# Gate products on 32 columns of the array, the latent by halves of the tokens on 64 columns, and an order of the work drawn per stretch of steps

## The chip, the cores and the metric

The kernel runs on one core of a Trainium2 chip. It uses five engines: TensorE (PE in the profile; its weight loads are listed apart as PEld), VectorE (DVE), ScalarE (ACT), GpSimd (POOL), and SyncE (SP), which only issues transfers here. The metric is the device time in microseconds of one execution; lower is better. A time is the median of several executions, and one more execution is recorded by the hardware profiler.

## The reference

Eight sequences of 512 tokens with 256 features go through four residual layers, all in float32:

```
x = x + attention_a(layernorm(x));  x = x + ffn(layernorm(x))
x = x + retention_b(layernorm(x));  x = x + ffn(layernorm(x))

attention_a:  q = x Wq + bq;  latent = x Wd + bd  (64 wide);  k, v = latent Wup + bup;  16 heads of 16, rope on q and k
   out = softmax(q k' / 4 + distance terms) v
   out = out + 0.2 * sigmoid(q . mean_k) * mean_v        # mean over the 512 tokens
   return out Wo + bo
retention_b:  q, k, v = projections;  return ((q k') * decay) v        # no softmax
ffn:          relu(x W1 + b1) W2 + b2                                   # 1024 wide
```

## The kernel before, in words

**Layout.** The tokens of a sequence are 4 tiles of 128 (`NT`), the features 2 chunks of 128 (`NC`). The heads are handled in 4 groups of 4 (`NG`); a head takes 32 partitions, 16 for its dimensions and the rest for helper rows, so that four heads fill the array's rows.

**Front of a sequence.** `front1` and `front2` normalise x, turn it (`xT`), and make the `lat` tile, keys, queries and values from it. In the kernel before, `latent` multiplies with the weights `wd_sb` laid out twice side by side, so that the 64 latent features stand on partitions 0 to 63 and once more on 64 to 127, both for all 512 tokens. The keys (`k`) read one copy per half of the head dimension (`e`), the values (`v`) one copy per odd and even token tile; so two matmuls of 64 rows can stand side by side on the array's rows. `half_unit` adds bias and rope on VectorE, `rotate` combines the halves on GpSimd, `stripes` copies them by transfers of SP into `qT` and `kT`. `mean_k` writes `kmean`, `gate` multiplies `kmean` (16 useful columns of 128) with the rotated queries and writes tanh of it into 16 rows of `gates`. `mean_v` and `through_wo` make `mem`, 17 rows: what each head's mean value gives behind Wo, and a row of constants. `wo_unit` adds `gates` times `mem` to the output projection. (sigmoid is written with tanh, so a constant row of ones in `gates` carries the rest.)

**Attention steps.** There are 256 steps, 32 per sequence, and 6 more that close the pipeline. One step multiplies scores of two heads twice: `s` (queries on partitions, for the row maxima, read by VectorE into `mr`) and, 12 steps behind (`LAG`), `t` (keys on partitions, read by ScalarE's exp into `p`). The decay factors `dec_a` are multiplied on GpSimd, or VectorE where the planner says so. `pv` multiplies `p` with the values, on 32 columns per head. The tiles `s` and `t` share two PSUM buffers.

**The rest of a sequence** (`rest`, `rest_last`): output projection (`wo`), the feed-forward layers (`hx` up, `x` down), retention (`b`, `bv`, `bs`, `bo`), with three layer norms (f, r, g).

**What sets the order.** Every engine runs its instructions in program order. `plan` (a function at build time) writes that order: it keeps a clock for each engine, takes the costs from the `Unit` objects (`Unit(latent, 1720, ...)`: 1720 ns of TensorE, then 700 ns of ScalarE, and so on), and puts units of work between the steps. It is run for 144 rules (reserve, lateness and so on); the rule with the smallest cost is emitted. It adds 1700 ns to a plan's cost for each wait of TensorE over 1200 ns, and during the first two sequences fills waits over 700 ns with matmuls that nothing uses (`warm`).

Lines L69 and L203 in the profile are the helpers that record instructions (`traced` and `mm`), L206 is `flip` (turns on TensorE), L93 is `move` (transfers of SP).

Of the kernel before, what the change touches and what calls it, by code (L numbers as in the profile page):

```python
# [35 lines left out]
def tile_kernel(  # L36
# [80 lines left out]
    wd_sb = keep([P, NC, 2, LAT], "wd_sb")  # L117
    for j in range(2):
        move(wd_sb[:, :, j, :], wdown)
# [30 lines left out]

    gates = [keep([P, T], f"ga{i}") for i in range(2)]
    mem = [keep([P, D], f"me{i}") for i in range(2)]
    bo_row = keep([32, D], "bo_row")
    kmean = keep([P, 2, P], "kmean")
    vmean = keep([P, NC, P], "vmean")
    hmask = keep([P, NH], "hmask")
    vmask = keep([P, NC, NH + 1], "vmask")
# [3 lines left out]
    def memory_buffers():  # L161
        for i in range(2):
            gps.memset(gates[i], 0.0)
            gps.memset(mem[i], 0.0)
        gps.memset(bo_row, 0.0)
        gps.memset(vmean, 0.0)
        gps.memset(vmask, 0.0)
        gps.memset(vmask[:, :, NH : NH + 1], 1.0)
        gps.memset(kmean, 0.0)

    def masks():
        dve.reduce_sum(hmask, ident.rearrange("p (h d) -> p h d", d=HH), axis=AX.X)
        for c in range(NC):
            dve.reduce_sum(
                vmask[:, c, c * HH : (c + 1) * HH], ident.rearrange("p (h d) -> p h d", d=HD), axis=AX.X
            )
        gps.tensor_scalar(hmask, hmask, 0.5 / T, None, ALU.mult)

    late = {}

    def loads_before_scores():
        xs[1] = load_x(1)
        late["dec_a"] = resident(decay_a, "dec_a")
        for i in range(2):
            move(gates[i][NH : NH + 1, :], rope[HD : HD + 1, 0, :])
        move(bvc, rows[0:D].rearrange("(c p) -> p c", p=P))

    def late_loads():
        move(bo_row[NH : NH + 1, :], rows[D : 2 * D].unsqueeze(0))

        for g in range(NG):
            at_row = (g % 2) * 4 * HD
            move(wo_sb[at_row : at_row + 4 * HD, g // 2, :], wo.rearrange("(h d) g n -> h d g n", d=32)[:, :HD, g, :])

        move(wvu[:, :, :D], wb[:, :, 2, :])
        late["w1"] = resident(w1, "w1_sb")
        late["w2"] = resident(w2, "w2_sb")
        late["dec_b"] = resident(decay_b, "dec_b")
# [21 lines left out]
    wk_sb = keep([P, P], "wk_sb")  # L220

    def regroup_k():
        for e in range(2):
            act.copy(
                wk_sb[e * LAT : (e + 1) * LAT, :].rearrange("p (h d) -> p h d", d=HH),
                wk_in[e * LAT : (e + 1) * LAT, :, e * HH : (e + 1) * HH],
            )
# [8 lines left out]
    pick = keep([P, 2, 32], "pick")  # L236
# [20 lines left out]
    AHEAD = 6  # L257
# [152 lines left out]
    def front1(b):  # L410
        def latent(part=0, parts=1):
            if part == 0:
                lat_a[b] = fr.tile([P, T], F32, tag="lat", name=f"lat_{b}")
                lsum[b] = fr.tile([P, 2], F32, tag="lsum", bufs=1, name=f"lsum_{b}")
            ps = misc(f"lat_{b}_{part}")
            n = T // parts
            cols = slice(part * n, (part + 1) * n)
            for c in range(NC):
                mm(ps[:, :n], wd_sb[:, c].rearrange("p j n -> p (j n)"), xT_a[b]["xT"][:, c, cols], c == 0, c == NC - 1)
            act.activation(  # L420
                lat_a[b][:, cols], ps[:, :n], AF.Identity,
                bias=bd, accum_out=lsum[b][:, part : part + 1],
            )
            if part == 1:
                gps.tensor_add(lsum[b][:, 0:1], lsum[b][:, 0:1], lsum[b][:, 1:2])
# [3 lines left out]
        def values():  # L429
            ps = [misc(f"v_{b}_{j}") for j in range(2)]  # L430
            for i in range(2):
                for j in range(2):
                    rows_of = slice(j * LAT, (j + 1) * LAT)
                    t = 2 * i + j
                    mm(ps[j][:, i * D : (i + 1) * D], lat_a[b][rows_of, t * P : (t + 1) * P], wv_sb[rows_of])
            for j in range(2):
                act.copy(
                    vaug[b % 2][:, j::2, : NH * 17].rearrange("p i (h d) -> p i h d", d=17)[:, :, :, :HD],
                    ps[j].rearrange("p (i h d) -> p i h d", i=2, d=HD),
                )  # L440


        def mean_v():
            ps = misc(f"mv_{b}")
            for c in range(NC):
                mm(ps[:, c : c + 1], wv_sb[:LAT, c * P : (c + 1) * P], lsum[b][:LAT, 0:1])
            m = fr.tile([P, NC], F32, tag="mv_a", name=f"mv_a_{b}")
            dve.scalar_tensor_tensor(m, ps[:, :NC], 0.1 / T, bvc, ALU.mult, ALU.add)
            for c in range(NC):
                gps.tensor_scalar(vmean[:, c, : NH + 1], vmask[:, c, :], m[:, c : c + 1], None, ALU.mult)  # L450

        def bias_through_wo():
            ps = misc("bo")
            for c in range(NC):
                mm(ps[:, :D], vmean[:, c, :], wo_sb[:, c, :], c == 0, c == NC - 1)
            dve.tensor_add(bo_row[: NH + 1, :], ps[: NH + 1, :D], bo_row[: NH + 1, :])

        def through_wo():
            ps = misc(f"me_{b}")
            for c in range(NC):  # L460
                mm(ps[:, :D], vmean[:, c, :], wo_sb[:, c, :], c == 0, c == NC - 1)
            dve.tensor_add(mem[b % 2][: NH + 1, :], ps[: NH + 1, :D], bo_row[: NH + 1, :])

        s, (h0, h1) = ln_units(lambda: xs[b], f"a{b}", fr)
        u = {"lat": Unit(latent, 1720, (("ACT", 700),), after=[h0[2], h1[2]]), "latent": latent}
# [16 lines left out]
    def front2(b, u1):  # L482
# [3 lines left out]
        def projected(j, e):  # L486
            ps = misc(f"{'qk'[j]}{e}_{b}")
            if j == 0:
                for c in range(NC):
                    mm(ps, wq_sb[:, c, e, :], xT_a[b]["xT"][:, c, :], c == 0, c == NC - 1)  # L490
            else:
                rows_of = slice(e * LAT, (e + 1) * LAT)
                mm(ps, wk_sb[rows_of], lat_a[b][rows_of])
            return ps

        def keys():
            ps = [projected(1, e) for e in range(2)]
            for e in range(2):
                half_unit(1, e, ps[e])

        def half_unit(j, e, ps, order="cs"):
            for n in order:
                table = cos if n == "c" else nsin
                if b == 0 and (j, e) == (0, 1):
                    if not spare:
                        spare["t"] = at.tile([P, 2, T], F32, tag="p", bufs=PB, name="rq1_0")
                    t = spare["t"][:, "cs".index(n), :]
                else:
                    t = fr.tile([P, T], F32, tag="rot", bufs=6, name=f"r{n}{j}{e}_{b}")
                dve.scalar_tensor_tensor(t, ps, qk_bias[:, j, e : e + 1], table, ALU.add, ALU.mult)  # L510
                rot[n, j, e] = t
# [28 lines left out]
        def gate():  # L540
            ps = misc(f"ga_{b}")
            for e in range(2):
                mm(ps, kmean[:, e, :], rot[0, e], e == 0, e == 1)
            act.activation(gates[b % 2][:NH, :], ps[:NH, :], AF.Tanh)
# [4 lines left out]
        k = [Unit(keys, 950, rope + rope, after=[lat], bank=2)]  # L549
        kt = Unit(lambda: turn(1), then=(("POOL", 2800),), after=k, step=free)  # L550
        km = Unit(mean_k, then=(("ACT", 1300), ("POOL", 1400)), after=[kt])
        q = [Unit(lambda e=e: half_unit(0, e, projected(0, e)), 1720, rope, after=[lat]) for e in range(2)]
        qt = Unit(lambda: turn(0), then=(("POOL", 2800),), after=q, gives=("qk", b))
        ga = Unit(gate, 1720, (("ACT", 600),), after=[km, qt], needs=(("wo", b - 2),))
# [5 lines left out]
        if b == 0:  # L560
            return projected, half_unit, rotate, stripes, [km, u1["v"], ga, u1["mv"], u1["me"]]
# [465 lines left out]
    projected, half_unit, rotate, stripes, order0 = front2(0, front[0][1])  # L1027
# [20 lines left out]
    latent(0, 2), latent(1, 2)  # L1048
    regroup_k()
    regroup_q(1)  # L1050
    half_unit(0, 0, projected(0, 0))
    k_ps = [projected(1, e) for e in range(2)]
    half_unit(1, 0, k_ps[0]), half_unit(1, 1, k_ps[1], "sc")
    rotate(1, 0, gps), rotate(1, 1, gps)
    half_unit(0, 1, projected(0, 1), "sc")
# [8 lines left out]
    gps.tensor_copy(vmean[:, :, NH], bvc)  # L1064
# [7 lines left out]
    def plan(reserve, later, early, fast, lead, bias, emit=False):  # L1072
# [196 lines left out]
        valued, drawn = [0], [0]  # L1269
        shifts, posts = [], []  # L1270
# [36 lines left out]
        while t < LAST or any(chains) or posts or shifts or valued[0] < NS:  # L1307
            while True:
# [7 lines left out]
                for c, u in ready:  # L1316
                    if (u is c[0] or u.norm) and start_of(u) is not None:
                        c.remove(u)
                        issue(u)
            s_step = step_start(t) if t < LAST else None  # L1320
# [4 lines left out]
            for rank, c in enumerate([shifts, posts] + chains):  # L1325
# [11 lines left out]
                if t >= LAST:  # L1337
                    key = (max(s - (BONUS if c is last_two[0] or c is last_two[1] else 0), clock["PE"] + 50), -rank)
                if best is None or key < best[0]:
# [24 lines left out]
            if best is not None and not take:  # L1364
                soon = clock["PE"] + 50
                take = (best[1] is posts or best[1] is shifts or credit > 0) and best[2] <= max(soon, s_step)
# [28 lines left out]
    plan(*min(rules, key=cost.get), emit=True)  # L1395
# [109 lines left out]
```

## Time and profile before

| what | value |
|---|---|
| median of 3 runs (lowest, highest) | 1268.3 us (1267.91, 1269.02) |
| the profiled execution's own time | 1267.68 us |
| its span, first to last instruction | 1265.9 us |
| its mean granted TensorE clock | 0.995 |
| HBM read, written | 13.92 MB, 4.43 MB |

The profile's first part gives busy time per engine, its second cuts the span into 40 slices with the busy share in tenths, its fourth follows the chain of work that ended last, its fifth groups instructions by tile. In the trace a float32 matmul stands as two passes (records), so a group's count is twice the number of matmuls; a matmul that turns a tile (L206) is one pass. The timeline view gives start, length, engine, operation and count, with the wait ahead of it in brackets.

### The profile page before, as it was taken

To read this page: it belongs to the slowest core of one execution; us is meant where nothing else is said; L and a number is where in the kernel's file an instruction comes from. 1 tells how busy PE (TensorE), PEld (TensorE's weight loads), DVE (VectorE), ACT (ScalarE), POOL (GpSimd) and SP (SyncE) were. 2 spreads that over 40 slices of the span, in tenths; PEclk is the share of its full clock that TensorE was granted. 3 is DMA by queue.
4 is the path that set the end of the run, shared out by engine and by line. 5 is a ranking of instruction groups with operands and counts; after the bars stand their busy time and mean duration, and the time that the engine had idled before them with its cause. 6 is when DMAs were issued, how large, how long until landed. Compare 5 with 4: busy or idle time off the path is not lost.

```text
span 1265.9 us, 15939 instructions
## 1 busy us (share of the span) xinstructions
PE 1225.4 (97%) x6168; PEld 628.8 (50%) x6168; DVE 615.4 (49%) x995; ACT 499.4 (39%) x746; POOL 763.6 (60%) x699
## 2 busy tenths in 40 slices
PE   7989999999998999999999999999999999999999
PEld 5423445344534344455443644535543554467777
DVE  4777854573544663345734365433634372232410
ACT  2245444444453434334335245343434334523131
POOL 4379965795766876676657576675656564731210
PEclk9999999999999999999999999999999999999999
DMA  5310010002100100010000200011000100000000
GB/s 136 117 39 23 23 38 6 14 7 56 29 14 5 49 23 18 18 48 23 1 14 5 66 22 14 1 31 41 4 5 14 31 5 5 26 1 1 1 5 30
DMA packets 32728, 31.94 MB, mean 25 GB/s; under 512 B 14065, under 2 KB 23538, under 8 KB 32372
## 3 DMA queue, kind: packets, MB, share of 16 engines
q1 hardware_dynamic: 31740, 30.13, 8.7%
q8 instruction: 49, 0.80, 0.3%
q10 hardware_dynamic: 912, 0.79, 0.2%
q14 instruction: 27, 0.22, 0.1%
HBM read 13.92 MB, written 4.43 MB: 14 GB/s over the span
## 4 chain that ended last, share of the span: by engine, by line
PE 88%; DVE 6%; POOL 2%; DMA 2%; ACT 1%; issue 1%; SPq 0%; ACTq 0%; DVEq 0%
PE hx L203 19%; PE s L203 18%; PE x L203 18%; PE pv L203 8%; PE wo L203 3%; PE bs L203 3%; PE bo L203 3%; DVE mr L69 3%; PE b L203 2%; PE bv L203 2%; PE q L203 2%; POOL p L69 2%; PE t L203 2%; PE warm L203 1%; PE lat L203 1%; PE ga L203 1%
## 5 line engine op out<-in xcount | busy, mean ns | idle before, releaser
L69 POOL TENSOR_TENSOR p<-p,dec_a 128x512 f32<-128x512 f32 x482 | 610.0, 1290 | 296.5 <-ACT p L69 290.1
L69 DVE TENSOR_REDUCE mr<-s 128x2 f32<-128x1024 f32 x256 | 312.7, 1223 | 314.0 <-PE t L203 291.6
L69 ACT ACTIVATE p<-t 128x1024 f32<-128x1024 f32 (+1 forms) x282 | 263.0, 944 | 366.0 <-PE t L203 356.3
L203 PE MATMUL s<-kT,qT 32*128 32x512 f32 x1024 | 289.3, 640 | 19.5 <-DVE mr L69 17.0
L203 PE MATMUL t<-qT,kT 32*128 32x512 f32 x1024 | 287.2, 641 | 0.5 <-ACT p L69 0.3
L203 PE MATMUL x<-w_sb,h_x 128*128 128x256 f32 x960 | 221.0, 384 | 0.0
L203 PEld LDWEIGHTS x<-w_sb,h_x 128*128 128x128 f32 x960 | 178.3, 190 | 59.4 <-issue 36.4
L203 PEld LDWEIGHTS s<-kT,qT 32*128 32x128 f32 x1024 | 78.0, 183 | 162.0 <-DVE mr L69 62.9
L203 PE MATMUL pv<-p,va 128*32 128x512 f32 x1024 | 132.8, 608 | 1.6 <-ACT num L69 0.7
L69 ACT ACTIVATE h_x<-hx,vec 128x512 f32<-128x512 f32 (+1 forms) x128 | 84.5, 660 | 109.2 <-PE hx L203 108.3
L203 PE MATMUL hx<-xT_f,w_sb 128*128 128x512 f32 (+1 forms) x288 | 122.1, 560 | 0.2 <-ACT xT_f L69 0.2
L203 PE MATMUL hx<-xT_g,w_sb 128*128 128x512 f32 (+1 forms) x288 | 122.0, 560 | 0.0
L69 DVE TENSOR_TENSOR x<-x,x 128x256 f32<-128x256 f32 x60 | 25.5, 425 | 153.2 <-PE x L203 145.7
L203 PEld LDWEIGHTS t<-qT,kT 32*128 32x128 f32 x1024 | 78.6, 183 | 14.2 <-ACT p L69 5.4
L203 PEld LDWEIGHTS hx<-xT_g,w_sb 128*128 128x128 f32 x288 | 51.2, 189 | 64.0 <-issue 60.1
L203 PEld LDWEIGHTS hx<-xT_f,w_sb 128*128 128x128 f32 x288 | 50.8, 189 | 64.3 <-issue 55.3
L203 PEld LDWEIGHTS pv<-p,va 128*32 128x32 f32 x1024 | 25.3, 109 | 77.1 <-issue 51.5
L69 POOL TENSOR_TENSOR x<-x,b 128x256 f32<-128x256 f32 x60 | 43.9, 754 | 14.7 <-DVE xn_g L69 11.6
L69 POOL TENSOR_TENSOR rc<-rc,rs 128x512 f32<-128x512 f32 x30 | 40.2, 1361 | 9.2 <-DVE rs L69 9.2
L69 DVE TENSOR_TENSOR p<-p,dec_a 128x512 f32<-128x512 f32 x30 | 35.7, 1227 | 18.1 <-ACT p L69 18.1
L69 POOL TENSOR_TENSOR rstd_g<-ve_g,half 128x2 f32<-128x2 f32 x16 | 11.3, 704 | 54.0 <-DVE ve_g L69 53.8
L69 ACT COPY num<-pv 128x512 f32<-128x512 f32 x32 | 18.7, 585 | 57.9 <-PE pv L203 53.4
(172 smaller groups left out, 1103.0 us busy)
## 6 DMA issues: line engine op xcount, KB each, us to landing
kT<-rc SPq DMA_DIRECT2D x64, 64.0 KB
qT<-rc SPq DMA_DIRECT2D x60, 64.0 KB
x<-in_x_dram SPq DMA_DIRECT2D x7, 512.0 KB
aT<-num SPq DMA_DIRECT2D x112, 32.0 KB
rec<-d_rec SPq DMA_DIRECT2D x14, 256.0 KB
out_dram<-x SPq DMA_DIRECT2D x28, 128.0 KB
w_sb<-in_w_dram SPq DMA_DIRECT2D x2, 1024.0 KB
x<-in_x_dram SPq DMA_DIRECT2D x2, 256.0 KB
```

Of the source, the lines that this page charges most:

```text
L69: ins = f(*a, **k)
L203: tc.keep_in_program_order(nc.tensor.matmul(o, lhsT=l, rhs=r, start=start, stop=stop))
```

## The change

It has four parts.

1. **Latent.** `wd_sb` is held once instead of twice. For each chunk, two matmuls of 256 tokens stand on 64 columns each: the first half of the tokens goes to partitions 0 to 63, the second half to 64 to 127. `lat` is 256 wide instead of 512. The keys are made by `projected_keys`: four matmuls of 256 columns (two `e` by two token halves) instead of two of 512, and each key tile is read from two PSUM tiles, so `half_unit` runs twice as many VectorE instructions of half the width for keys. Sums for mean v come from one accumulator column on 128 partitions, so an addition on GpSimd falls away. The first sequence keeps its two parts, one per half of the tokens.
2. **Gate.** `kmean` has 32 columns. `gate` issues eight matmuls of 128 tokens (two `e` by four token tiles), each token tile on its own 32 columns, instead of two of 512 tokens on 128 columns; then four tanh of 32 partitions by 128 columns instead of one of 16 by 512. `gates` becomes block-diagonal by token tile, and `mem`, `vmask`, `vmean`, `bo_row` hold their 17 rows four times. The constant ones come from the bias of tanh (`one_rows`: 40 in that row) instead of a transfer into each gate tile.
3. **Planner's costs.** Latent 1050 instead of 1720 ns, gate 620 instead of 1720, keys one entry of 3500 ns on VectorE instead of two of 1550, the ScalarE parts of latent and gate 480 and 900 instead of 700 and 600.
4. **Draws.** After the best rule is found, each stretch of 16 steps (`min(t, LAST) // 16`, 17 stretches) is given a number from 1 to 6 in turn, which seeds a random generator. Where a stretch has one, candidates' start times get 0, 400 or 1500 ns added by chance (0 three times in five), and the threshold of the credit that lets work in before a step gets 0, 1500 or -1500. A number is kept if the planner's cost of the whole plan falls. The emitted plan uses the kept numbers.

In the program as built, the number of matmuls per kind stays the same except for `lat` (18 to 32), `k` (16 to 32), `ga` (16 to 64) and `warm` (76 to 92). 482 decay products are on GpSimd and 30 on VectorE in both.

```
-    wd_sb = keep([P, NC, 2, LAT], "wd_sb")
-    for j in range(2):
-        move(wd_sb[:, :, j, :], wdown)
+    wd_sb = keep([P, NC, LAT], "wd_sb")
+    move(wd_sb, wdown)
...
+    one_rows = keep([P, 4], "one_rows")
-    kmean = keep([P, 2, P], "kmean")
+    kmean = keep([P, 2, 32], "kmean")
-    vmask = keep([P, NC, NH + 1], "vmask")
+    vmask = keep([P, NC, NT, 32], "vmask")
...
     def loads_before_scores():
         xs[1] = load_x(1)
         late["dec_a"] = resident(decay_a, "dec_a")
-        for i in range(2):
-            move(gates[i][NH : NH + 1, :], rope[HD : HD + 1, 0, :])
+        move(one_rows, blocks[:, P : P + 4])
...
-        def latent(part=0, parts=1):
-            if part == 0:
-                lat_a[b] = fr.tile([P, T], F32, tag="lat", name=f"lat_{b}")
-                lsum[b] = fr.tile([P, 2], F32, tag="lsum", bufs=1, name=f"lsum_{b}")
-            ps = misc(f"lat_{b}_{part}")
-            n = T // parts
-            cols = slice(part * n, (part + 1) * n)
+        def latent(parts=(0, 1)):
+            if parts[0] == 0:
+                lat_a[b] = fr.tile([P, T // 2], F32, tag="lat", name=f"lat_{b}")
+                lsum[b] = fr.tile([P, 1], F32, tag="lsum", bufs=1, name=f"lsum_{b}")
+            ps = misc(f"lat_{b}_{parts[0]}")
+            n = T // 2
             for c in range(NC):
-                mm(ps[:, :n], wd_sb[:, c].rearrange("p j n -> p (j n)"), xT_a[b]["xT"][:, c, cols], c == 0, c == NC - 1)
-            act.activation(
-                lat_a[b][:, cols], ps[:, :n], AF.Identity,
-                bias=bd, accum_out=lsum[b][:, part : part + 1],
-            )
-            if part == 1:
-                gps.tensor_add(lsum[b][:, 0:1], lsum[b][:, 0:1], lsum[b][:, 1:2])
+                for j in parts:
+                    mm(
+                        ps[j * LAT : (j + 1) * LAT, :n], wd_sb[:, c, :], xT_a[b]["xT"][:, c, j * n : (j + 1) * n],
+                        c == 0, c == NC - 1,
+                    )
+            at_ = slice(parts[0] * LAT, (parts[-1] + 1) * LAT)
+            act.activation(lat_a[b][at_], ps[at_, :n], AF.Identity, bias=bd[at_], accum_out=lsum[b][at_])
...
             for c in range(NC):
-                gps.tensor_scalar(vmean[:, c, : NH + 1], vmask[:, c, :], m[:, c : c + 1], None, ALU.mult)
+                gps.tensor_scalar(vmean[:, c, :], vmask[:, c].rearrange("p t h -> p (t h)"), m[:, c : c + 1], None, ALU.mult)
...
-        u = {"lat": Unit(latent, 1720, (("ACT", 700),), after=[h0[2], h1[2]]), "latent": latent}
+        u = {"lat": Unit(latent, 1050, (("ACT", 480),), after=[h0[2], h1[2]]), "latent": latent}
...
-            else:
-                rows_of = slice(e * LAT, (e + 1) * LAT)
-                mm(ps, wk_sb[rows_of], lat_a[b][rows_of])
...
+        def projected_keys():
+            ps = [misc(f"k{j}_{b}") for j in range(2)]
+            n = T // 2
+            for e in range(2):
+                for j in range(2):
+                    rows_of = slice(j * LAT, (j + 1) * LAT)
+                    mm(ps[j][:, e * n : (e + 1) * n], wk_sb[rows_of, e, :], lat_a[b][rows_of])
+            return [[p[:, e * n : (e + 1) * n] for p in ps] for e in range(2)]
...
-                dve.scalar_tensor_tensor(t, ps, qk_bias[:, j, e : e + 1], table, ALU.add, ALU.mult)
+                parts = ps if j else [ps]
+                for i, part in enumerate(parts):
+                    at_ = slice(i * T // len(parts), (i + 1) * T // len(parts))
+                    dve.scalar_tensor_tensor(t[:, at_], part, qk_bias[:, j, e : e + 1], table[:, at_], ALU.add, ALU.mult)
...
             for e in range(2):
-                mm(ps, kmean[:, e, :], rot[0, e], e == 0, e == 1)
-            act.activation(gates[b % 2][:NH, :], ps[:NH, :], AF.Tanh)
+                for t in range(NT):
+                    mm(
+                        ps[t * 32 : t * 32 + 32, :P], kmean[:, e, :], rot[0, e][:, t * P : (t + 1) * P],
+                        e == 0, e == 1,
+                    )
+            for t in range(NT):
+                own = slice(t * 32, t * 32 + 32)
+                act.activation(gates[b % 2][own, t * P : (t + 1) * P], ps[own, :P], AF.Tanh, bias=one_rows[own, 0:1])
...
-        k = [Unit(keys, 950, rope + rope, after=[lat], bank=2)]
+        k = [Unit(keys, 950, (("DVE", 3500),), after=[lat], bank=2)]
-        ga = Unit(gate, 1720, (("ACT", 600),), after=[km, qt], needs=(("wo", b - 2),))
+        ga = Unit(gate, 620, (("ACT", 900),), after=[km, qt], needs=(("wo", b - 2),))
...
+    gps.tensor_scalar(one_rows, one_rows, 40.0, None, ALU.mult)
+    dve.reduce_sum(one_rows[:, 0:1], one_rows, axis=AX.X)
...
+            k = min(t, LAST) // 16
+            if k != drawn_for[0]:
+                drawn_for[0] = k
+                bent[0] = random.Random(97 * k + draws[k]) if k < len(draws) and draws[k] else None
+            bend = (lambda *a: bent[0].choice(a)) if bent[0] else (lambda *a: a[0])
...
+                key = (key[0] + bend(0, 0, 0, 400, 1500), key[1])
...
-                take = (best[1] is posts or best[1] is shifts or credit > 0) and best[2] <= max(soon, s_step)
+                take = (best[1] is posts or best[1] is shifts or credit > bend(0, 0, 0, 1500, -1500)) and best[2] <= max(soon, s_step)
...
-    plan(*min(rules, key=cost.get), emit=True)
+    rule = min(rules, key=cost.get)
+    draws, least = [0] * (NS // 16 + 1), cost[rule]
+    for k in range(len(draws)):
+        for n in range(1, DRAWS + 1):
+            tried = draws[:k] + [n] + draws[k + 1 :]
+            c = plan(*rule, tried)
+            if c < least:
+                draws, least = tried, c
+    plan(*rule, draws, emit=True)
```

## The prediction

> **What bounds the kernel now.** I read busy shares and the chain first, then stages, then what TensorE waits for, and last single rows of the timeline.
>
> ```profile
> PE 1225.4 (97%) x6168; PEld 628.8 (50%) x6168; DVE 615.4 (49%) x995; ACT 499.4 (39%) x746; POOL 763.6 (60%) x699
> ...
> PE 88%; DVE 6%; POOL 2%; DMA 2%; ACT 1%; issue 1%; SPq 0%; ACTq 0%; DVEq 0%
> ```
>
> TensorE is busy for 97% of the span and is 88% of the chain. Two stages, before and after 239 us (columns: stretch, its length, busy us per engine, granted clock):
>
> ```profile
> 54.70:239.00 184.30, 172.72 (x930) 72.79 (x929) 121.67 (x173) 85.20 (x142) 138.20 (x120) 0.99 0.09 23
> 239.00:1266.00 1027.00, 1005.57 (x4986) 527.66 (x4984) 464.58 (x780) 401.90 (x568) 608.14 (x546) 1.00 0.07 19
> ```
>
> After 239 us TensorE is idle for 21.4 of 1027 us: a microsecond of its work saved there is nearly one of time. Before, 11.6 of 184.3 us are idle. The waits and the two-column-group rows of the timeline:
>
> ```profile
> PE s L203 <- DVE mr L69: 17.0, 22, 2.1
> ```
>
> ```profile
> 488.93 1.07 PE L203 MATMUL pv<-p,va 128*32 128x512 f32 x8
> 489.93 1.98 PE L203 MATMUL hx<-xT_g,w_sb 128*128 128x512 f32 x4
> ...
> 517.39 1.92 PE L203 MATMUL pv<-p,va 128*32 128x512 f32 x16
> 519.25 0.70 PE L203 MATMUL s<-kT,qT 32*128 32x512 f32 x2
> ...
> 557.56 1.13 PE L203 MATMUL v<-wv_sb,lat 64*128 64x256 f32 x8
> 558.62 0.70 PE L203 MATMUL s<-kT,qT 32*128 32x512 f32 x2
> ```
>
> A block costs the distance to the next start. Eight `pv` passes take 1.00 us, sixteen 1.86: 0.86 per eight (0.107 each) and 0.14 for the change of tile shape. Four passes alone on 128 columns (`hx`) take 1.81 to 1.91. So four tiles of 32 columns run at once.
>
> ```profile
> 743.35 1.98 PE L203 MATMUL ga<-rc,kmean 128*128 128x512 f32 x4
> 745.27 0.70 PE L203 MATMUL s<-kT,qT 32*128 32x512 f32 x2
> ...
> 769.62 1.98 PE L203 MATMUL lat<-xT_a,wd_sb 128*128 128x512 f32 x4
> 771.44 0.60 PE L206 MATMUL tr_g<-ident,xn_g 128*128 128x128 f32 x4
> ```
>
> **Gate (8 times).** Before: 745.27 - 743.35 = 1.92 us. After: 16 passes of 128 instead of 512 columns, four at a time: 16 x 0.107 / 4 = 0.43, plus 0.14: 0.57. Saved 1.35 each, 10.6 in all with 0.1 off twice where work on 128 columns stands ahead. Bounds: without overlap a pass of 128 columns is 0.107 alone, 16 make 1.71, and nearly nothing is saved; a floor per pass comes from the shortest passes shown, `qk_bias` on 32 columns of the array (one column moved, 32 passes):
>
> ```profile
> 4.81 0.84 PE L203 MATMUL qk_bias<-vec,pick 128*32 128x1 f32 x32
> 5.58 1.60 PE L203 MATMUL warm<-ident 128*128 128x128 f32 x12
> ```
>
> 0.77 / 32 = 0.024 us a pass, below the 0.027 that I use, so the floor does not bind. [...]
>
> **Latent (7 times).** Before 1.82 to 1.91. After: eight passes of 256 columns, two tiles of 64 columns at once. No row has 64 columns; the nearest is `v`, eight passes of 256 with two tiles of 64 rows: 1.06. Saved 0.8 each, 5.6 in all; 0 if columns of 64 do not overlap. Sequence 0 issues its halves apart and saves nothing.
>
> **Other work of TensorE.** Keys: twice the matmuls, half the width, still two at a time: 1.06 before and after. `warm` rises from 76 to 92, only in waits.
>
> **Where it counts.** Gate 0 stands among warm matmuls that pace the first steps: 1.25 in full. Between 54.7 and 239 us lie gates 1 and 2 and latents 1 to 3. Gate 2 (171 us) and latent 3 (226 us) stand where TensorE is 96% and more busy: 2.15. The other three (2.95) stand where it is 85 to 90% and GpSimd up to 88% (46.75 of 53 us from 85 to 138): half, 1.45; bounds 0 and 2.95. Gates 3 to 7 and latents 4 to 7 come after 239 us: 6.65 + 3.2 = 9.85. Sum 14.7.
>
> **What they covered.** A score step's buffer is free only when VectorE has reduced it:
>
> ```profile
> 244.72 0.70 PE L203 MATMUL s<-kT,qT 32*128 32x512 f32 x2 [0.25 <-DVE mr L69]
> ...
> 247.18 0.70 PE L203 MATMUL s<-kT,qT 32*128 32x512 f32 x2 [0.25 <-DVE mr L69]
> ```
>
> So steps cannot start closer than 2.46 us; a step takes 1.07, and what stands between must fill 1.39. A latent of 1.06 or a gate of 0.57 alone no longer does. Over the built orders, single short blocks after 239 us fall short of 2.46 by 9.2 us in all before and 9.8 after (among them two latents and one keys block alone): 0.6 lost.
>
> **Keys on VectorE.** Four instructions of 128x512 (0.74 us each, 0.66 apart) become eight of 128x256; the nearest row is `ret` of 128x256, 0.475 us, so some 0.42 apart: 3.4 us instead of 2.6. Behind them on VectorE's queue stands the next step's reduction, and for that waits the step after. In the built order sequence 3's keys are followed by four turns, a step, four `pv` matmuls and a turn: 0.53 + 1.07 + 1.1 + 0.1 = 2.8 us, while keys and reduction need 0.3 + 3.4 + 1.2 = 4.9: a wait of 2.1, where before two `b` blocks stood there and no wait followed. Sequence 4's: 4.1 against 4.9, 0.8. The 0.26 that before waits right behind sequence 3's key product goes, since turns now stand there. I take 2.6 us lost; bounds 0 and 5.8 (7 x 0.83, every sequence exposed).
>
> **Costed at nothing.** Four tanh (0.26 each by the `neg` row, 16x128) for one of 0.585: 0.45 us more on ScalarE, 39% busy; the output projection needs them only in the next sequence's time; exposed at worst 8 x 0.45 = 3.6. `vmean` 128 wide instead of 17: 0.459 to at most 0.75 on GpSimd, 60% busy, two instructions ahead of `me` only: at worst 0.6 x 8. Start: the chain goes from the second `wd_sb` load to that of `wq_in` (start, length):
>
> ```profile
> 2.97 2.63 DMA wd_sb<-in_wdown_dram
> 5.62 8.68 DMA wq_in<-in_wq_dram
> ```
>
> The second load goes, and SP issued it 0.7 us after the first, so the first `q` product may come 0.7 earlier; the keys' VectorE run puts 0.6 back; `one_rows` lands like `bvc` (31.1 us, waited for on GpSimd) and the first reduction, at 33.6, stands behind it on VectorE. SP's queue has two transfers fewer in all. I take 0, bounds -0.7 and +0.9.
>
> **Order.** The draws move nearly every unit; engines and counts stay. Every wait of TensorE after 239 us adds up to 21.4 us; I see no place in the built order that decides more than those named, and take 0, bounds -9 and +9 (two fifths of it, either way).
>
> **Sum.** 14.7 - 0.6 - 2.6 = 11.5 us. Against the profiled execution, 1267.7 - 11.5 = 1256.2; it lay 0.6 below the median of 1268.3, so 1256.8.
>
> **Rivals.**
> (1) Better order as well: a third or more of the 21.4 us of waits goes: 1244 to 1251. For: the kept draws were chosen where the plan's clocks show less waiting. Against: 17.0 us of the waits are score steps on reductions, and keys now hold VectorE longer.
> (2) The gain is handed back: keys exposed in all sequences (3.2 more), latents without overlap (5.6 more), tanh exposed (3.6): 1262 to 1269. For: DVE is already what steps wait for. Against: `v` and `pv` rows show overlap both ways.
> (3) Slower, by one mechanism: waits near 2 us in the new order that bring a stretch of half clock.
>
> ```profile
> 1041.65 0.70 PE L203 MATMUL s<-kT,qT 32*128 32x512 f32 x2 [2.12 <-DVE mr L69]
> ...
> 1043.08 1.94 PE L203 MATMUL pv<-p,va 128*32 128x512 f32 x8
> ```
>
> ```profile
> 1041.30:1044.70 3.40, 3.05 (x16) 0.51 (x16) 2.56 (x4) 2.00 (x3) 3.40 (x4) 0.65 0.05 11
> ```
>
> After the wait, `pv`'s eight passes take 1.87 instead of 1.00, a step 1.43 instead of 1.07, and the stretch has a granted clock of 0.65. One such event costs 2.1 + 0.87 + 0.36, with the wait ahead of it (0.62) some 4.0 us. Three more, and the gain is gone within 0.2%; from four more on (15.9) the kernel is slower, 1272.7 and up. The trace has three after the start (75.4, 1041, 1188 us). [...]
>
> **Chances.** Forecast 1251 to 1262: 0.60. (1): 0.13. (2): 0.17, most of it still faster, a third of it within 0.2%. (3): 0.10, eight in ten of it slower. A median of these runs tells 0.2% (2.5 us) from no change. Faster 0.85, within 0.2% 0.07, slower 0.08. The range 1246 to 1265 leaves out (3), half of (1) and the top of (2), some 0.2.
>
> **What would show it.** `ga` x128 passes with blocks of some 0.57 us, and `lat` on 128*64 with 1.06; busy TensorE down by some 15 us without `warm`; waits of score steps on reductions up by 2 to 3 us, one near 2 us behind sequence 3's keys. Wrong if `lat` blocks stay at 1.8, if more half-clock stretches than three follow the start, or if the waits on reductions exceed 25 us.

## The result, and the profile after

The changed kernel took 1262.17 us (median of 14 runs, 1250.43 to 1266.40) beside 1267.40 us for the kernel before (14 runs, 1264.80 to 1269.13): a ratio of 0.9938, interval 0.9911 to 0.9965. Two later measurements gave 1255.91 us (0.9917, 0.9885 to 0.9949) and 1254.82 us (0.9895, 0.9867 to 0.9922). Over all 28 runs (two of them single executions, further down) the median is 1257.7 us, between 1249.9 and 1266.4; over the 43 runs of before that stand beside them it is 1267.7, between 1263.4 and 1270.2. So some 10 us were won, and the runs of one and the same program came to differ by 16 us. The second fact is the larger part of this study.

The page after, busy time and shares of the chain of waits (this execution took 1254.66 us, span 1252.9; the text calls it the first profile):

```profile
PE 1209.3 (97%) x6356; PEld 628.9 (50%) x6356; DVE 625.8 (50%) x1030; ACT 500.7 (40%) x765; POOL 767.5 (61%) x703
...
PE 87%; DVE 9%; DMA 1%; issue 1%; POOL 1%; ACT 1%; SPq 0%; DVEq 0%; ACTq 0%
```

TensorE still sets the time; it is busy 16.1 us less (19.8 without the unused `warm` matmuls, which rose from 22.7 to 26.4), and VectorE's share of the chain rose from 6 to 9%. The changed blocks in the timeline of TensorE:

```profile
451.44 0.65 PE L205 MATMUL ga<-rc,kmean 128*32 128x128 f32 x16
452.01 0.70 PE L205 MATMUL s<-kT,qT 32*128 32x512 f32 x2
...
474.89 1.08 PE L205 MATMUL lat<-xT_a,wd_sb 128*64 128x256 f32 x8
475.90 0.66 PE L208 MATMUL tr_f<-ident,xn_f 128*128 128x128 f32 x4
```

From start to start a gate takes 0.57 us and a latent 1.01. The two stages again (stretch, its length, busy us of each engine, granted clock):

```profile
52.80:228.50 175.70, 163.41 (x1002) 72.99 (x1000) 117.50 (x182) 85.98 (x147) 141.57 (x122) 0.99 0.08 21
228.50:1252.90 1024.40, 1000.60 (x5089) 527.71 (x5088) 478.64 (x801) 401.77 (x579) 608.32 (x545) 1.00 0.07 19
```

The first stage, of the same steps as before to half a step, is 8.6 us shorter, the second only 2.6 (1027.0 before), though 9.85 us of TensorE's work went there. Its idle time grew from 21.4 to 23.8 us. The waits of TensorE (in all, times, longest):

```profile
PE s L205 <- DVE mr L70: 20.1, 28, 2.9
...
PE mx L208 <- DVE mr L70: 3.5, 6, 2.0
```

### The profile page after: what moved, and what is told of

It reads as the page before. It is cut to its first block, busy times and chain, and to the rows that moved or that the text cites. A ratio compares the mean times of both kernels' runs of the same rounds, so it can differ in the third digit from the quotient of the medians.

```text
span 1252.9 us, 16351 instructions
## 1 busy us (share of the span) xinstructions
PE 1209.3 (97%) x6356; PEld 628.9 (50%) x6356; DVE 625.8 (50%) x1030; ACT 500.7 (40%) x765; POOL 767.5 (61%) x703
## 4 chain that ended last, share of the span: by engine, by line
PE 87%; DVE 9%; DMA 1%; issue 1%; POOL 1%; ACT 1%; SPq 0%; DVEq 0%; ACTq 0%
PE s L205 19%; PE x L205 18%; PE hx L205 18%; PE pv L205 8%; DVE mr L70 4%; PE bs L205 3%; PE wo L205 3%; PE bo L205 3%; PE b L205 2%; PE bv L205 2%; PE q L205 2%; PE t L205 2%; PE warm L205 2%; DVE p L70 2%; DMA wq_in<-in_wq_dram 1%
## 5 line engine op out<-in xcount | busy, mean ns | idle before, releaser
L205 PE MATMUL s<-kT,qT 32*128 32x512 f32 x1024 | 290.3, 644 | 20.2 <-DVE mr L70 20.1
L70 DVE TENSOR_TENSOR p<-p,dec_a 128x512 f32<-128x512 f32 x30 | 39.1, 1343 | 18.8 <-ACT p L70 18.7
```

The lines of the kernel that those rows point to most:

```text
L70: ins = f(*a, **k)
L205: tc.keep_in_program_order(nc.tensor.matmul(o, lhsT=l, rhs=r, start=start, stop=stop))
```

## The experiments

### The forms and the order, apart

The forms of gate, latent and keys, and the order that the planner writes, can be exchanged. "Half clock" in what follows is a stretch in which the trace's granted clock of TensorE is 0.50. Four kernels were measured beside 17 runs of before (median 1267.69 us). The changed kernel once more:

> The changed kernel as it is, for its spread and one more profile. Runs of it lay between 1250.4 and 1266.4 us, those of the kernel before between 1264.8 and 1269.1. Theory 'half clock': a run's time follows the number of 3.41 us stretches at half clock; one stretch takes 0.0014 off the mean granted clock and adds some 1.2 to 1.7 us, so runs near 1251 have a clock of 0.995 or more and runs near 1265 one of 0.984 to 0.988. Rival 'contention': times spread without the clock, as GpSimd and VectorE get in each other's way differently from run to run; then clock and time are not related.

The new forms in the order of before, which keeps the old costs and draws nothing (the cost lines shortened):

```
-    AHEAD, DRAWS = 6, 6
+    AHEAD, DRAWS = 6, 0
-    Unit(latent, 1050, (("ACT", 480),), ...)   Unit(keys, 950, (("DVE", 3500),), ...)   Unit(gate, 620, (("ACT", 900),), ...)
+    Unit(latent, 1720, (("ACT", 700),), ...)   Unit(keys, 950, rope + rope, ...)        Unit(gate, 1720, (("ACT", 600),), ...)
```

> The new latent, keys and gate, but the old costs in the planner and no draws, so that the units stand in the very order of the kernel before. Theory 'work': the gain is TensorE's removed work, 8 gates x 1.35 and 7 latents x 0.8 = 16 us less what the shorter blocks and the longer key instructions on VectorE hand back (2 to 5): 1252 to 1257. Theory 'order': the gain comes from the drawn order, and the new forms alone give at most 4 us: 1263 to 1267. If the spread of the changed kernel comes from its forms, it shows here too (over 10 us); if from its order, these runs spread by under 6 us.

The old forms in the order of the changed kernel: the kernel before with the new costs and the draws (the same lines the other way round).

> The old latent, keys and gate, with the new costs in the planner and the draws, so that the units stand in the very order of the changed kernel. Theory 'work': no gain, 1265 to 1272, since the order is neutral and the old blocks are long again. Theory 'order': 1255 to 1262. A spread of over 10 us here says that the order brings it, under 6 that the forms do.

The changed kernel without draws (new forms and costs, `DRAWS = 0`, the best rule's order as it is):

> The changed kernel without its draws: new forms and new costs, the best of the 144 rules as it is. Theory 'work': 1252 to 1258, like the changed kernel's own runs without extra half-clock stretches. Theory 'order': the draws carry the gain, 1262 to 1268.

| kernel | median us (lowest, highest; runs) | ratio to before, interval | profiled span, clock |
|---|---|---|---|
| changed, again | 1255.91 (1250.04, 1262.51; 6) | 0.9917, 0.9885 to 0.9949 | 1251.8, 0.995 |
| new forms, old order | 1259.84 (1259.12, 1261.64; 5) | 0.9942, 0.9930 to 0.9953 | 1259.6, 0.991 |
| old forms, new order | 1265.14 (1261.21, 1269.33; 12) | 0.9981, 0.9967 to 0.9996 | 1259.4, 0.997 |
| new forms, no draws | 1276.94 (1275.71, 1278.09; 5) | 1.0073, 1.0061 to 1.0085 | 1276.3, 0.987 |

The forms are worth 7.9 us in the old order and 9.2 in the new one, the order 2.5 with old forms and 3.9 with new ones. The figures of 9.2 and 3.9 rest on six runs that spread by 12.5 us; with the median of all 28 they are 7.4 and 2.1. The new costs without the draws make the kernel slower than before. Several expectations were missed: 1259.84 lies between the two ranges for the new forms in the old order, 1276.94 above both for the kernel without draws, and the spread of 8.1 us with old forms decides nothing. The spread of 2.5 us with the new forms in the old order points, as was laid down for it, to the new order and not the forms alone as what brings the wide spread.

Since the second kernel issues the same blocks of TensorE in the same order as before, the two traces can be laid side by side, start to start. The eight gates gave 10.06 us, the seven latents 5.4. The span fell by 6.3. What went back lies mostly in stretches of half clock and in the wait ahead of one of them, for the exponential.

First the place in the kernel before, then the same place with the new forms (TensorE alone):

```profile
469.57 1.13 PE L203 MATMUL s<-kT,qT 32*128 32x512 f32 x4 [2.41 <-ACT p L69]
...
471.20 1.98 PE L203 MATMUL hx<-xT_g,w_sb 128*128 128x512 f32 x4
473.12 1.07 PE L203 MATMUL pv<-p,va 128*32 128x512 f32 x8
```

```profile
456.45 0.64 PE L205 MATMUL ga<-rc,kmean 128*32 128x128 f32 x16
457.02 0.61 PE L205 MATMUL mv<-lsum,wv_sb 128*128 128x1 f32 x4
457.49 1.96 PE L205 MATMUL hx<-xT_g,w_sb 128*128 128x512 f32 x4
463.42 1.22 PE L205 MATMUL s<-kT,qT 32*128 32x512 f32 x2 [3.97 <-ACT p L70]
...
466.00 3.53 PE L205 MATMUL hx<-xT_g,w_sb 128*128 128x512 f32 x4
469.46 1.07 PE L205 MATMUL pv<-p,va 128*32 128x512 f32 x8
```

Before, this wait was 2.41 us and no half clock followed: the wait rose by 1.56 us, the gate ahead of it had become 1.34 shorter. Then `hx` took 3.46 us to the next start instead of 1.92. Between 457 and 469.5 us, 4.0 us were given back. The windows at this place and two others (clock 0.50):

```profile
462.30:469.10 6.80, 5.68 (x12) 2.17 (x12) 5.05 (x12) 5.10 (x10) 6.80 (x9) 0.50 0.00 0
588.60:595.40 6.80, 6.80 (x18) 2.49 (x17) 2.78 (x4) 1.02 (x1) 5.52 (x6) 0.50 0.00 1
...
168.80:172.20 3.40, 3.30 (x16) 1.01 (x16) 1.72 (x3) 2.08 (x4) 3.40 (x6) 0.50 0.00 0
```

In all this trace has 23.9 us of half clock against 13.7 in that of before (at a clock of 0.50 a microsecond of it costs at most a half, an estimate).

The kernel without draws waits 24.1 us for reductions, and has one place that shows how a queue in order passes a delay on:

```profile
495.06 0.39 SPq L94 DMA_DIRECT2D x<-in_x_dram  x1
...
498.98 0.75 DVE L70 BATCH_NORM_STATS2 st_a<-x 128x6 f32<-128x256 f32 x2 [3.94 <-DMA x<-in_x_dram]
...
500.06 0.16 DVE L70 SCALAR_TENSOR_TENSOR nm_f<-mv_f,rstd_f 128x2 f32<-128x2 f32 x1
...
500.25 1.10 ACT L70 ACTIVATE xn_f<-x,nm_f,rstd_f 128x256 f32<-128x256 f32 x2 [7.55 <-DVE nm_f L70]
...
500.90 1.39 PE L208 MATMUL tr_f<-ident,xn_f 128*128 128x128 f32 x4 [3.42 <-ACT xn_f L70]
```

The next sequence's statistics stand on VectorE's queue ahead of `nm_f`, an instruction of 0.16 us, and wait 3.94 us for a load; ScalarE waits for `nm_f`, TensorE for ScalarE, and 13.65 us of half clock follow (500.2 to 513.9 us). In the changed kernel's profile TensorE has no wait for `xn_f`.

### Two weak places of the changed order

Behind the start, the first profile after showed two places with waits of nearly 2 and 3 us. One is the reduction behind sequence 3's keys. Timeline, VectorE and TensorE:

```profile
225.32 0.87 DVE L70 SCALAR_TENSOR_TENSOR rc<-k,qk_bias,rope_sb 128x256 f32<-128x256 f32 x2
...
226.10 0.87 DVE L70 SCALAR_TENSOR_TENSOR rs<-k,qk_bias,rope_sb 128x256 f32<-128x256 f32 x2
...
226.88 1.22 DVE L70 TENSOR_REDUCE mr<-s 128x2 f32<-128x1024 f32 x1
...
228.25 0.27 PE L208 MATMUL mx<-ident,mr 128*16 128x128 f32 x1 [1.95 <-DVE mr L70]
...
230.53 1.94 PE L205 MATMUL pv<-p,va 128*32 128x512 f32 x8
```

Eight instructions of the keys (four of them shown) hold the reduction up until 226.88; the turn `mx` waits 1.95 us, and the `pv` block behind it runs at half the clock (1.87 us to the next start instead of 1.00). The other place was not foreseen at all:

```profile
281.44 2.48 POOL L70 TENSOR_TENSOR p<-p,dec_a 128x512 f32<-128x512 f32 x2
...
283.39 6.57 DVE L70 TENSOR_TENSOR p<-p,dec_a 128x512 f32<-128x512 f32 x2
...
283.89 2.48 POOL L70 TENSOR_TENSOR rc<-rc,rs 128x512 f32<-128x512 f32 x2
...
284.51 3.70 PE L205 MATMUL hx<-xT_g,w_sb 128*128 128x512 f32 x8
...
286.34 2.47 POOL L70 TENSOR_TENSOR p<-p,dec_a 128x512 f32<-128x512 f32 x2
...
289.88 1.21 DVE L70 TENSOR_REDUCE mr<-s 128x2 f32<-128x1024 f32 x1
...
291.15 1.22 PE L205 MATMUL s<-kT,qT 32*128 32x512 f32 x2 [2.94 <-DVE mr L70]
```

Two decay products of step item 68, given to VectorE, took 6.57 us (the first of them 5.97) while GpSimd ran six instructions of 1.2 us one behind the other (four products and the two of `rc`); the reduction behind them came late, a step waited 2.94 us, and half clock followed. Against the old forms in the same order, where the same pair took 2.77 us, TensorE loses 4.6 us here in the first profile of the changed kernel, and 5.8 in the second (the execution of 1253.56 us).

Three kernels mend one or both, without a change in TensorE's order, and a fourth takes other random numbers. Item 68 on GpSimd:

```
-        eng = gps if pooled[n] else dve
+        eng = gps if pooled[n] or n == 68 else dve
```

> The changed kernel with one difference: the two decay products of score item 68 (at 283 us, 6.57 us on VectorE beside GpSimd's products) run on GpSimd. TensorE's order is the same. Theory A (VectorE's products were held up by GpSimd's own run of four, the reduction behind them came 5 us late, and a half-clock stretch followed): the step after them starts some 3 us earlier, the stretch at 291 us goes, the span to the closing falls by 4 to 6 us, the profiled span is 1246 to 1249 and the median 1249 to 1258. Rival B (the steps there wait for something else as well): no more than 1 us is gained and the median stays at 1255 to 1262.

The keys' eight instructions, four ahead of the next reduction and four behind it:

```
-            for e in range(2):
-                half_unit(1, e, ps[e])
+            half_unit(1, 0, ps[0])
+            behind.append([lambda: half_unit(1, 1, ps[1]), 1])
...
                     f(k, ps)
+                    if f is reduce_item:
+                        catch_up()
...
```

(`catch_up` issues what `behind` holds: behind the next reduction, or earlier where a turn of the keys or a PSUM tile needs it.)

> The changed kernel with the keys' eight VectorE instructions split: four ahead of the next step's reduction, four behind it, in each of the seven sequences. TensorE's order is the same. Theory A (the eight instructions of 3.1 us hold the reduction up; predicted at 2.6 us in all): the wait of 1.95 us behind sequence 3's keys falls under 0.6, the half-clock stretch at 229.7 us mostly goes, 2 to 3 us are gained. Rival B (the four instructions behind the reduction hold the next one up in the same way, or the two banks that the keys keep longer stall TensorE): the wait moves to the next step and the time is the same within 1 us.

Both:

> Both of the two differences. If they are independent: 6 to 9 us under the changed kernel, profiled span 1243 to 1246, median 1245 to 1254, and the spread of its runs smaller than the changed kernel's 16 us, since two places that fall to half the clock in some runs are gone. If the spread has its cause in the other weak places (405, 455, 570, 620 us), it stays above 8 us.

Other draws, `random.Random(1009 * k + 31 + draws[k])` for `random.Random(97 * k + draws[k])`:

> The changed kernel with other random numbers behind its draws (as many draws, the same acceptance). The draws took 21 us off (1276.9 without them). If they are a draw among orders whose real times scatter, this lands anywhere from 1250 to 1275, and its waits on reductions lie at other places than 223 and 283 us; if the search reliably finds the weak places of the first order, it lands within 4 us of 1256 to 1262.

| kernel | median us (lowest, highest; runs) | ratio to before (1268.05), interval | profiled span, clock |
|---|---|---|---|
| item 68 on GpSimd | 1249.99 (1248.48, 1251.51; 4) | 0.9857, 0.9845 to 0.9870 | 1248.6, 0.996 |
| keys' halves apart | 1253.17 (1247.22, 1256.58; 6) | 0.9877, 0.9854 to 0.9899 | 1253.0, 0.990 |
| both | 1251.03 (1249.53, 1253.25; 4) | 0.9867, 0.9854 to 0.9880 | 1249.0, 0.993 |
| other draws | 1252.22 (1249.45, 1257.57; 4) | 0.9868, 0.9850 to 0.9885 | 1255.8, 0.989 |

All four are faster than the kernel before by 1.2 to 1.4%, and the first is the best version measured; its median also lies below the three of the changed kernel (1254.8 to 1262.2), though no run of that one stood beside it on this chip. Each mend does at its place what was expected: with item 68 moved, the `hx` block at 284 us is followed after 3.63 us by the next step, not 6.64:

```profile
284.23 3.70 PE L205 MATMUL hx<-xT_g,w_sb 128*128 128x512 f32 x8
287.86 0.70 PE L205 MATMUL s<-kT,qT 32*128 32x512 f32 x2
```

This gain at its place is no proof of one in the median, though: in the profiles of the changed kernel at 1249.95, 1263.32 and 1266.02 us item 68 was not held up at all. With the keys apart, the line of `mx` becomes

```profile
228.06 1.23 DVE L70 TENSOR_REDUCE mr<-s 128x2 f32<-128x1024 f32 x1
...
229.44 0.27 PE L208 MATMUL mx<-ident,mr 128*16 128x128 f32 x1 [0.41 <-DVE mr L70]
```

and the times of the two do not add up: both together are no faster than item 68 alone, and their profiled span of 1249.0 us misses the 1243 to 1246 that was expected. The keys' mend has the lowest single run of all, 1247.22 us at a granted clock of 0.999, and others of 1255 to 1257 at 0.988 to 0.990. Its gain is not shown in the median. The other draws don't have the place of item 68, and behind sequence 3's keys `mx` waits 1.27 us instead of 1.95 (at 233 us); their median fits a search that finds weak places as well as a scatter among orders, so this run doesn't tell the two apart.

### Where the 16 us between runs lie

Each run lists its granted clock, and the changed kernel's times follow it, though not strictly: 1250.43 us at 0.997, 1254.66 at 0.993, 1262.28 at 0.988, 1265.95 at 0.984, but also 1256.53 at 0.996. Two more profiles of the unchanged program were taken, to have one of the longer runs in a trace.

> The changed kernel as it is, one more profiled execution. Its single runs lie in two groups, 1250 to 1257 us at a granted clock of 0.992 to 0.997 and 1262 to 1266 us at 0.984 to 0.988, and both profiles so far are of the first group. Theory A (the second group is the same work with more half-clock stretches): a profile of the second group shows eight to eleven stretches of 3.4 us where the first shows four or five, most of them in a row after one of the weak places (223 to 233, 283 to 293, 400 to 408, 566 to 575 us), the same waits before them, and span times clock within 2 us of the other profiles' 1244 to 1246. Rival B (the second group has a longer wait somewhere, a transfer or VectorE's products): span times clock is 5 us or more above, and one wait of over 4 us stands in it.

> As for the look before it: the changed kernel once more, to have both groups of its runs in profiles. If it falls in the first group (1250 to 1257 us) it shows whether the product of 6.57 us at 283 us comes in each execution (theory: a matter of the order in which VectorE and GpSimd come to it, the same in each run of one program) or only in some.

They took 1266.02 and 1263.32 us (spans 1264.2 and 1261.5, clocks 0.984 and 0.985). Both show the rival's long wait (4.9 us) and the theory's half clock (12 and 11 times 3.41 us), one behind the other; span times clock, 1244.0 and 1242.6, stays near the others' 1244 to 1246, as the theory and not the rival had it. First the timeline of an execution of 1249.95 us (the control further down), at item 13:

```profile
91.31 3.55 DVE L70 TENSOR_TENSOR p<-p,dec_a 128x512 f32<-128x512 f32 x2
91.37 2.94 POOL L70 TENSOR_TENSOR rc<-rc,rs 128x512 f32<-128x512 f32 x2
...
94.27 5.40 POOL L70 TENSOR_TENSOR p<-p,dec_a 128x512 f32<-128x512 f32 x4
94.37 1.18 PE L205 MATMUL pv<-p,va 128*32 128x512 f32 x5
```

Then the same instructions in the execution of 1266.02 us:

```profile
94.35 8.60 DVE L70 TENSOR_TENSOR p<-p,dec_a 128x512 f32<-128x512 f32 x2
94.43 2.48 POOL L70 TENSOR_TENSOR rc<-rc,rs 128x512 f32<-128x512 f32 x2
...
96.88 4.92 POOL L70 TENSOR_TENSOR p<-p,dec_a 128x512 f32<-128x512 f32 x4
...
102.40 2.53 PE L205 MATMUL pv<-p,va 128*32 128x512 f32 x8 [4.93 <-DVE p L70]
```

and the windows of that execution, the wait and what follows it:

```profile
97.50:102.40 4.90, 0.00 (x0) 0.00 (x0) 4.90 (x2) 0.60 (x1) 4.30 (x4) 0.79 0.36 94
102.40:114.00 11.60, 10.29 (x52) 5.01 (x52) 6.71 (x9) 3.60 (x8) 2.21 (x3) 0.50 0.00 0
```

In the shorter execution VectorE and GpSimd take turns: VectorE's pair takes 3.55 us and GpSimd's products are longer too (5.40 for four instead of 4.92). In the longer one GpSimd runs six instructions (`rc` and `p`) at its full pace, and VectorE's first product, 8.00 us long, ends only when the sixth has ended. TensorE stands still for 4.9 us and then runs at half the clock until 114 us. In both VectorE starts 0.06 to 0.08 us ahead of GpSimd's next product; nothing in the two timelines says which of them will go first. (A third outcome stands in the execution of 1253.56 us: there VectorE goes first at this place, and its first product takes 0.68 us.) Laid side by side from start to start, the longer execution is 3.0 us behind at 91 us and 12.2 behind at 107; most of another 3.9 us lies in two stretches of half clock of 6.8 us at 414 and 582 us, where the shorter one has a single one of 3.4. The trace of the 1263.32 us execution has the same product of 8.00 us. Item 68's pair took 2.77 us in the 1266.02 us execution and 2.75 in that of 1249.95: long only in the two profiles of 1254.66 and 1253.56 us. So a product that is held up comes in some executions of one program and not in others, at two places.

Half clock in all, from the trace's record of the clock: 10.2 us in the execution of 1249.95 us, 17.1 in that of 1254.66, 37.6 and 41.0 in those of 1263.32 and 1266.02; 13.7 in the one of before.

Last, both items on GpSimd, beside the changed kernel as a control:

```
-        eng = gps if pooled[n] else dve
+        eng = gps if pooled[n] or n in (13, 68) else dve
```

> The changed kernel with the decay products of items 13 (at 92 us) and 68 (at 283 us) on GpSimd instead of VectorE; TensorE's order is the same. Beside the changed kernel itself on the same chip. Theory A (in the slower group of the changed kernel's runs VectorE's product of item 13 waits 8.0 us behind six GpSimd products, and the wait and its half clock are the 10 to 12 us between the groups): no run of this kernel lies in a second group, all within 6 us of each other; since GpSimd ends item 13's products some 2 to 4 us later than an undisturbed VectorE does, item 13 costs up to 3 us, item 68 saves 4 to 6: median 1248 to 1254. Rival B (the groups differ in another way, and the long product is only one sign of it): two groups 8 us or more apart are here as well.

> The changed kernel again, on the chip of the run before it. Theory A: again two groups, 1250 to 1257 and 1262 to 1266 us, median anywhere between. If this chip never shows the second group, all runs lie at 1250 to 1257, which makes the second group a matter of the chip, and the run before it tells nothing of its cause.

With both items moved the five runs lie between 1251.38 and 1255.86 us (median 1253.66; 0.9889, 0.9871 to 0.9906); the control's six between 1249.87 and 1262.33 (1254.82; 0.9895, 0.9867 to 0.9922). The spread falls from 12.5 to 4.5 us, as the theory had it, though only one of the control's six runs lies above 1257.2, so five runs without one prove little; the medians don't differ measurably: GpSimd ends item 13's products later than an undisturbed VectorE, and at item 13 the trace loses 2.7 us against the control's (from 0.3 ahead at 93 us to 2.4 behind at 104, part of it in a half-clock stretch at 100.6). Of the changed kernel's 28 runs 13 lie at 1262 us or above; of 13 runs of the three kernels with item 68 on GpSimd, none. What the longer two executions lost at item 13 is shown; that item 13 causes the longer runs in general is argued from these two profiles and this one comparison of eleven runs. Open remains why the three kernels of the same order with item 13 still on VectorE (14 runs, on another chip) showed no run over 1257 us either, and what decides which engine goes first.

## Why the prediction was right

1256.8 us were predicted; between the medians of all runs 10.0 us less was measured (11.5 predicted). The terms for TensorE's work were right block by block; two others, the order and the clock, were off with opposite signs and nearly cancel. So it is in part luck that the sum came out within 1.5 us: the forms alone, for which it stands, brought 7.9 us in the old order. The first measurement alone (1262.17) touches rival (2)'s range, but not by its mechanisms: one sequence's keys were exposed, not all, latents overlap, and the tanh are hidden.

- **Gate.** Predicted 0.57 us a block and 10.6 in all; measured 0.57, and 10.1 and 10.6 over eight blocks (new forms against old, in the old and the new order). The floor of 0.024 us a pass, from the `qk_bias` row, did not bind: with 0.14 us for the change of tile shape a pass takes (0.57 - 0.14) / 16 = 0.027 us, the estimate worked out from `pv`.
- **Latent.** Predicted 1.06 and 5.6; measured 1.01, and 5.4 and 5.3 in all. Two tiles of 64 columns run side by side: eight passes of 256 columns take those 1.01 us, where four of 512 took 1.82 to 1.91.
- **Where it counts.** This step failed. The sum had 9.85 us of TensorE's work behind the score step that starts at 239.13 us before, of which short blocks and the keys of sequence 4 were to take 1.4. In the old order the new forms gain 7.0 us ahead of the start of that step, and lose 0.7 behind it (profiles of 1261.40 and 1267.68 us). In the new order, against the old forms' profile of 1261.21 us, the five profiles of the changed kernel gain 0.0, -0.3, 3.9, 1.5 and -0.4 us behind it (in the order 1254.66, 1253.56, 1249.95, 1266.02, 1263.32). A microsecond of work saved there was not one of time: in the old order 17.1 us of half clock instead of 6.8 (at most 5.1 us of time) and the longer wait for the exponential (1.6) take most of it back, in the first two profiles of the new one item 68 (4.6 and 5.8).
- **Short blocks.** Predicted 0.6; two latents (220.0 and 346.5 us) last 0.37 us longer for the next step's buffer: 0.74.
- **Keys on VectorE.** Sequence 3's wait was predicted at 2.1 and is 1.95. Of 2.6 in all, the kernel with the keys apart takes back 1.6 of `mx`'s waits (3.5 to 1.9) and 0.9 of the steps' (16.6 in the control to 15.7): 2.5. Right in the waits; in the median no gain is shown.
- **Costed at nothing.** A tanh takes 0.36 us, not 0.26, so a gate holds ScalarE 0.8 us longer, not 0.45; TensorE waits for it once, 0.4 us. `vmean` takes 0.76 (bound 0.75), and `me` waits 0.6 us in all, 0.9 before (1.7 with the new forms in the old order). The first score step starts at 31.8 us instead of 32.4, inside the bounds.
- **Order, taken as 0 with bounds of 9 either way.** Measured 2.5 us with old forms (0.5 to 4.2 by the interval) and 2.1 to 3.9 with new ones. Rival (1) was right in its direction, at a third of its size. That the wide bounds were due is shown by the kernel without draws, 21 us slower than the changed one.
- **What was missing.** The sum had no term for the clock outside of rival (3). That rival has the right mechanism: half clock came behind waits of 1.95, 2.94, 3.97 and 4.93 us, though not behind the one of 2.41 in the kernel before. Such an event gave back 4.0 us with the new forms in the old order, behind a wait for ScalarE. In the new order the largest events came from a source not looked at, products on VectorE held up by GpSimd's, and cost 4.6 to 5.8 us (item 68) and 9.2 us (item 13) where they came, not 4.0; they come only in some executions. Of the signs named, the rise of the steps' waits came (17.0 to 20.1 us), TensorE's busy time without `warm` fell by 19.8 us, not 15, and one sign of an error came: four half-clock stretches followed the start in the first profile, not three.
- **Waits near 2 us.** Rival (3) stood on one row, a clock of 0.65 behind a wait of 2.12 us. The wait of 1.95 us behind sequence 3's keys stood in seven profiled executions (all of the new order with new forms and the keys' instructions together), and half clock followed it in four. So the row was no single case, and such a wait does not bring half clock each time; what tells the four from the three stands in the last paragraph.

## What to carry to other kernels

When TensorE bounds a kernel, shorter blocks are worth what start-to-start distances say only as long as the waits around them neither grow nor bring the clock down (here 15.5 us by the blocks, 7.9 in the median): so lay two traces with the same order side by side, block by block, and list the stretches of half clock before explaining a difference. When single runs of one program differ, look for an instruction whose length differs between profiles, here a VectorE product beside a run of GpSimd products. A work list whose order comes from a planner should be measured with the old order as well, since the planner's costs alone moved this kernel by 17 us (1259.84 to 1276.94).

## What was not expected of the hardware

- **VectorE held up by GpSimd.** A VectorE product of two 128x512 tiles in SBUF takes 0.68 us alone, 1.7 to 1.9 when it takes turns with GpSimd's products (which rise from 1.26 to 1.72), and 5.97 or 8.00 where GpSimd goes on at its 1.26 each: it then waited until four and six of them were done. So VectorE can wait through a run of whole GpSimd instructions, in some executions and not in others; what holds it up is not shown by a trace. The planner counts 1.5 us for a pair of products on VectorE, and 0.8 more when GpSimd is busy.
- **The grid of the clock.** In these profiles stretches of half clock are 3.41, 6.83 or 13.65 us long, and within the first profile after their starts (14.6, 117.0, 229.7, 291.1, 407.2 us) lie 30, 33, 18 and 34 times 3.413 us apart. On this grid, continued from each profile's own stretches, the seven waits of 1.95 us part cleanly: the four that half clock followed lie wholly between two points of it (226.29 to 228.25 us between 226.26 and 229.67 in the first profile), the three others across one, as this one in the execution of 1266.02 us (239.19 to 241.14 us, across 240.32; no half clock follows, `pv` takes 0.99 us to the next start):

```profile
241.14 0.27 PE L208 MATMUL mx<-ident,mr 128*16 128x128 f32 x1 [1.95 <-DVE mr L70]
...
243.04 1.07 PE L205 MATMUL pv<-p,va 128*32 128x512 f32 x8
```

Of all 18 waits of TensorE of 1.9 to 2.2 us behind the first 40 us in the fourteen profiles, 13 lie wholly between two points, and half clock follows each of them; 5 lie across one, with 0.8 to 1.2 us on either side, and none follows. So in these profiles the same wait cost up to half of 3.41 us (an estimate, from the clock of 0.50) or nothing, by where it fell on the grid, which is another way in which the runs of one program come to differ.
